# Adapter's up product on two row halves, biases by VectorE, inverse begun by pairs, one pool for the experts' tiles

## The chip, the cores and the metric

The kernel runs on one core of one Trainium2 chip. The time is device microseconds for one execution of the whole program; the median of several executions is compared. All data are fp32. The engines are named as in the profile: PE (TensorE, matmuls; PEld are its weight loads), DVE (VectorE), ACT (ScalarE), POOL (GpSimd) and SP, which here only issues DMAs.

## The reference, cut to what matters

There are 16 batches of 1024 tokens with 256 features. A block of Nystrom attention is followed by a feed-forward with one expert per batch; each is added to the input after a layer norm.

```python
x = x + LN(attn(LN(x)))
x = x + LN(ffn(LN(x)))

# attn: 16 heads of 16 features, 64 landmarks per head
Q_l, K_l = landmark means of Q, K
kernel1, kernel2, kernel3 = softmax(Q K_l^T), softmax(Q_l K_l^T), softmax(Q_l K^T)
SV = (kernel1 @ iterative_inv(kernel2)) @ (kernel3 @ V);  out = SV @ w_proj

def iterative_inv(K):                       # K: 64x64 per head
    V = K^T / max over columns of sum over rows of K
    for _ in range(6):
        KV = K @ V
        V = 0.25 * V @ (13 I - KV @ (15 I - KV @ (7 I - KV)))
    return V

# ffn on x: 8 experts, hidden 64
base = x @ W_base + b_base      # sum over d of x[t, d] W_base[d, o]
losses = mean((relu(x Wd1[e] + bd1[e]) Wd2[e] + bd2[e] - x)^2)   # per batch and expert
idx = argmin(losses)                                             # one expert per batch
a = relu(x Wa_down[idx] + ba_down[idx])                          # 64 wide
y = base + a Wa_up[idx] + ba_up[idx]
```

The kernel folds the layer norms' means into centred weights: rows of w_proj, W_base and the chosen expert's up weights and biases have their mean subtracted (`centre`), so that only the mean square of y is left to be found.

## The kernel before, in words

Each batch goes through stages: *a* (norm, transposes `pt_a`, Q and K `pq`, V `pv`, kernel3's maxima `psm`, weights `psc` and products `put`, ending in `u`), *p* (kernel2 and its inverse), *c* (kernel1, attention output, projection `po`, residual `x`), *d1* (norm, transposes `pt_d`, the losses of eight experts, choice and gathers), *d2* (the chosen adapter and the output). There are four streams, one for each of a, p, c and d1+d2, and each runs through the batches in order.

The order in which the streams' steps are issued is found while the program is built, by a planner (`Model`, `planned`, lines 1134 to 1264). Each step says before its code what it will take: `mm(us, mode, n)` a piece on PE with its tile shape (`full`, `r32`, `q64` and others) and its count of PE instructions, `ew(engine, us, behind, mark)` a piece on another engine. With these the planner tries orders ahead and keeps the one that loses PE the least. PE, ACT, DVE and POOL then run their instructions in the emitted order; an engine that waits holds all that is behind it. PSUM is used as four buffers of two banks (`ps2`); a step takes one for each product and a piece marked `free` gives it back.

*Stage p* (lines 540 to 737). 16 heads of 64x64 lie as 8 pairs over 128 rows. `kp` spreads the landmark means by pair with a mask (4 DVE multiplications, L596), so that `pk` (L600) is two full matmuls of 256 columns; DVE takes the maxima and subtracts (L608, L610), ACT takes the exponent, DVE normalizes (L614 to L617). `pkt` turns the matrices with 64-square matmuls against an identity. The starting scale comes from sums of columns (`cs`, L625), a PE transpose (`pcs`, L628), a maximum and its reciprocal on 8 rows (L630 to L634) and a transpose back (`prd`, L637); then `vi` is scaled (L641). In the first iteration `pkv` multiplies (L678) and also transposes `vi` by the identity to get `vt` (L680, L686). `across` (L658) copies the parts of a matrix that are needed on the other half of the rows into a second tile of the same size.

*Stage d1* (lines 932 to 1059). Per batch 16 tiles `df` of 128x1024: PE makes `pr`, DVE subtracts x (L995), ACT squares and sums twice (L998). `df` has a pool of three buffers; `xn_d` and the outputs `y_d` have a pool `yd` of two. After the choice POOL issues five gathers with the row numbers in `row` (L1040): two for `wdn`, one for `bdn`, and for `wup` 64 rows of up weights and two copies of the expert's bias row. SP loads b_base as a further row of `wup` (L1056). DVE centres the 67 rows (L1058).

*Stage d2* (lines 1061 to 1096). `pad` is the down product, with the two halves of the tokens on the two halves of PSUM's rows; ACT puts both through relu into rows 0 to 63 of `a_t` (L1078). POOL fills rows 64 to 66 of `a_t` with 0.5, 0.5 and 1.0 (L1065, L1066), so that the bias rows of `wup` are added by the same matmul. Then, twice per batch, for four chunks of 128 tokens:

```python
for k in range(NC):
    nc.tensor.matmul(po[:, j, :], lhsT=xt[:, k, cols], rhs=wbase_sb[:, k, :], start=(k == 0), stop=False)
nc.tensor.matmul(po[:, j, :], lhsT=a_t[:, cols], rhs=wup, start=False, stop=True)
```

`taken` (L299) copies the result to SBUF on ACT (L302) and sums its squares there (L306); POOL makes the reciprocal root (L260, L262), DVE scales and adds the residual (L295), SP stores.

Of the kernel before, what the change touches and what calls it, by code (L numbers as in the profile page):

```python
# [8 lines left out]
F32 = mybir.dt.float32  # L9
# [6 lines left out]
P = 128  # L16
# [29 lines left out]
def kernel(  # L46
# [89 lines left out]
    bd1_rows = work.tile([E // 2, P], F32, tag="df", name="bd1_rows", bufs=3)  # L136
    nc.scalar.dma_start(out=bd1_rows, in_=bd1.rearrange("(i r) h -> i (r h)", r=2))
    bd2_rows = work.tile([E * NC, P], F32, tag="df", name="bd2_rows", bufs=3)
# [19 lines left out]
    nc.gpsimd.memset(ones, 1.0)  # L158
    nhalf = const.tile([P, 4], F32, name="nhalf")
# [8 lines left out]
    pairmask = groups("pairmask", PC)  # L168
# [130 lines left out]
    def taken(b, at, h, po, tag):  # L299

        y = buf4k(tag, [P, 4, D], f"y_{at}{b}_{h}")
        nc.scalar.copy(y, po)  # L302
# [19 lines left out]
    def stage_a(b):  # L322
# [39 lines left out]
        for t0 in range(0, NT, 4):  # L362
# [20 lines left out]
            if t0 == 0:  # L383
                yield go(
                    ("a", b, "bd"),
                    [("a", b, "qk", i, c) for i in range(2) for c in range(NC)] + ([("p", b - 1, "kp")] if b >= 1 else []),
# [153 lines left out]
    def stage_p(b):  # L540
# [23 lines left out]
        def product(dst, a, c, to, rest):  # L564
# [4 lines left out]
            for g0 in range(2):  # L569
                for g1 in range(2):  # L570
                    four = [h for h in heads if h[rest[0]] == g0 and h[rest[1]] == g1]
                    for h in sorted(four, key=lambda h: (h[frm] ^ h[to], h[frm])):
# [3 lines left out]
                        yt = y[h[y_at[0]] ^ h[y[2]]] if isinstance(y, tuple) else y  # L576
# [14 lines left out]

        yield step("kp", ew("dve", 0.8, None))
        lm, bd = live[b].pop("lm"), live[b]["bd"]
        kp = inv.tile([P, NC, PC, M], F32, tag="yx", name=f"kp_{b}")
        for p in range(PC):
            nc.vector.tensor_scalar(kp[:, :, p, :], lm[:, 1], pairmask[:, p : p + 1], None, ALU.mult)  # L596
        yield step("k2", mm(1.3, "full", 8), ew("dve", 1.25, -1, "free"), ew("act", 0.5))
        pk = one_bank([P, NP, M], f"pk_{b}")
        for c in range(NC):
            nc.tensor.matmul(  # L600
                pk[:, c * PC : (c + 1) * PC, :].rearrange("x p l -> x (p l)"),
                lhsT=bd[:, c, :, :].rearrange("f r l -> f (r l)"),
                rhs=kp[:, c].rearrange("f p l -> f (p l)"),
                start=True,
                stop=True,
            )
        mx = small.tile([P, NP], F32, tag="mx2", name=f"mx2_{b}", bufs=1)
        nc.vector.tensor_reduce(mx, pk, X, ALU.max)  # L608
        k2 = mat("vt", "k2")
        nc.vector.tensor_tensor(k2, pk, last(mx, M), ALU.subtract)  # L610
# [7 lines left out]
        yield step("k2t", mm(Q, "q64", 64), ew("act", 0.5, -1, "free"), ew("dve", 0.6))  # L618
# [20 lines left out]
        nc.scalar.copy(rd, prd)  # L639
        vi = mat("vi")  # L640
        nc.vector.tensor_tensor(vi, k2t, last(rd, M), ALU.mult)  # L641
        v_at = kt_at

# [667 lines left out]
```

## Time and profile before

| | |
|---|---|
| median of 6 runs | 2366.25 us (2361.93 to 2375.11) |
| the profiled execution's time | 2361.97 us |
| its span, first to last instruction | 2360.2 us |
| PE, DVE, ACT, POOL busy | 2161.2, 1425.0, 1317.8, 271.9 us |
| mean granted clock of PE | 0.98 |
| base matmuls of d2 (L1088) / up matmuls (L1089), busy | 134.9 / 78.2 us |
| y_d copies by ACT (L302), 32 | 32.4 us |
| fills of a_t by POOL (L1065, L1066), 16 each | 17.5 and 15.4 us |

Busy time of PE is the union of its matmuls. These are pipelined, and what one costs is seen best from the distance between starts. Idle time of an engine is told with what ended it.

### The profile page before, as it was taken

The numbers are of one execution on the slowest core, as the hardware profiler recorded it, in microseconds if no ns is written. First come the engines' busy times: TensorE is split into PE (matmuls) and PEld (weight loads), VectorE is DVE, ScalarE is ACT, GpSimd is POOL, SyncE is SP. The second block draws the span as 40 slices with busy tenths as digits, with TensorE's granted clock in tenths as the row PEclk, the third lists the DMA queues.
The fourth block names the chain that finished last, engine by engine and source line by source line (L and its number), as shares of the span: only waits on it lengthen the run. The fifth ranks groups of instructions, "written<-read, shape, count | busy, mean of one in ns | idle before, by whom it ended". The sixth has DMA issues, their size and how long they took to land.

```text
span 2360.2 us, 85848 instructions
## 1 busy us (share of the span) xinstructions
PE 2161.2 (92%) x39346; PEld 1381.3 (59%) x39346; DVE 1425.0 (60%) x2715; ACT 1317.8 (56%) x2659; POOL 271.9 (12%) x387
## 2 busy tenths in 40 slices
PE   7999999999899999999999999999999999898965
PEld 4666565565655766556565656657556465665542
DVE  6556565756456666665666667575665656475633
ACT  2345655645655556464665656565464655666635
POOL 1001020110200202021020200202011020111021
PEclk9999999999999999999999999999999999999878
DMA  3000001010010100101010010101001010010000
GB/s 112 20 21 21 2 20 41 5 56 2 13 47 3 58 2 14 46 5 55 2 58 2 14 46 3 58 2 48 12 5 56 2 40 2 6 38 20 22 21 21
DMA packets 56626, 60.36 MB, mean 26 GB/s; under 512 B 4996, under 2 KB 55240, under 8 KB 56264
## 3 DMA queue, kind: packets, MB, share of 16 engines
q1 hardware_dynamic: 50240, 50.35, 6.8%
q8 instruction: 309, 5.06, 0.9%
q0 software_dynamic: 2560, 2.14, 0.4%
q10 hardware_dynamic: 3464, 2.37, 0.3%
q14 instruction: 53, 0.43, 0.1%
HBM read 38.08 MB, written 16.78 MB: 23 GB/s over the span
## 4 chain that ended last, share of the span: by engine, by line
PE 41%; DVE 9%; ACT 7%; issue 3%; POOL 2%; DMA 0%; POOLq 0%; DVEq 0%; ACTq 0%
PE ph L954 6%; PE pq L351 5%; PE pr L987 4%; PE pf L1088 3%; ACT df L998 3%; PE po L881 3%; DVE df L995 2%; PE pf L1089 2%; PE pv L372 2%; PE psv L833 2%; PE psct L804 2%; PE psct L812 1%; PE psm L420 1%; PE pb L577 1%; PE psc L766 1%
## 5 line engine op out<-in xcount | busy, mean ns | idle before, releaser
L998 ACT ACTIVATE df<-df,bd_sb 128x512 f32<-128x512 f32 x512 | 363.2, 710 | 128.1 <-DVE df L995 127.1
L995 DVE TENSOR_TENSOR df<-pr,xt_d 128x1024 f32<-128x1024 f32 x256 | 302.8, 1217 | 83.6 <-PE pr L987 48.6
L987 PE MATMUL pr<-ht,wd_sb 64*64 64x512 f32 x2048 | 252.2, 597 | 6.8 <-ACT e L822 2.5
L954 PE MATMUL ph<-xt_d,wd_sb 128*128 128x512 f32 x512 | 238.1, 608 | 1.0 <-ACT e L822 0.7
L351 PE MATMUL pq<-xt_a,wqkv_sb 128*128 128x512 f32 x512 | 229.9, 599 | 0.0
L429 DVE TENSOR_REDUCE mx<-psm 128x2 f32<-128x1024 f32 x128 | 149.9, 1216 | 46.4 <-PE psm L420 46.2
L774 DVE TENSOR_REDUCE maxima<-psc 128x16 f32<-128x1024 f32 x128 | 150.1, 1215 | 27.6 <-PE psc L766 27.4
L954 PEld LDWEIGHTS ph<-xt_d,wd_sb 128*128 128x128 f32 x512 | 93.7, 192 | 115.8 <-issue 97.7
L822 ACT ACTIVATE e<-psct 128x1024 f32<-128x1024 f32 x128 | 123.5, 1016 | 66.9 <-PE psct L812 65.0
L351 PEld LDWEIGHTS pq<-xt_a,wqkv_sb 128*128 128x128 f32 x512 | 94.2, 190 | 108.2 <-issue 102.4
L465 ACT ACTIVATE e<-psc 128x1024 f32<-128x1024 f32 x128 | 122.7, 1021 | 32.9 <-PE psc L455 32.6
L1088 PE MATMUL pf<-wbase_sb,xt_d 128*128 128x256 f32 x512 | 134.9, 386 | 1.3 <-ACT xx L683 1.3
L881 PE MATMUL po<-wproj_sb,svt 128*128 128x256 f32 x512 | 122.1, 393 | 6.3 <-ACT vt L707 3.0
L260 POOL TENSOR_SCALAR ve_c_y<-ss_c 128x4 f32<-128x4 f32 x32 | 6.2, 195 | 1026.2 <-ACT square_c L306 1026.0
L692 DVE TENSOR_TENSOR sq<-psq,eye 128x512 f32<-128x512 f32 x96 | 65.8, 686 | 93.4 <-PE psq L577 88.5
L698 DVE TENSOR_TENSOR t<-eye,pb 128x512 f32<-128x512 f32 x96 | 65.4, 681 | 91.7 <-PE pb L577 91.4
L295 DVE SCALAR_TENSOR_TENSOR y_d<-y_d,rstd_d_y,x 128x256 f32<-128x256 f32 x128 | 53.2, 479 | 107.0 <-POOL rstd_d_y L262 107.0
L987 PEld LDWEIGHTS pr<-ht,wd_sb 64*64 64x64 f32 x2048 | 64.5, 133 | 89.4 <-issue 47.0
L372 PE MATMUL pv<-wqkv_sb,xt_a 128*128 128x256 f32 x512 | 116.6, 382 | 0.2 <-ACT e L822 0.2
L962 ACT ACTIVATE ht<-ph,bd_sb 128x1024 f32<-128x1024 f32 x64 | 71.0, 1109 | 75.0 <-PE ph L954 74.6
L881 PEld LDWEIGHTS po<-wproj_sb,svt 128*128 128x128 f32 x512 | 97.5, 195 | 25.3 <-ACT svt L856 4.1
L372 PEld LDWEIGHTS pv<-wqkv_sb,xt_a 128*128 128x128 f32 x512 | 95.6, 190 | 19.2 <-issue 5.0
(183 smaller groups left out, 4115.9 us busy)
## 6 DMA issues: line engine op xcount, KB each, us to landing
out_dram<-y_d SPq DMA_DIRECT2D x32, 512.0 KB
x<-in_L_attn_x_dram SPq DMA_DIRECT2D x15, 1024.0 KB
xa<-in_L_attn_x_dram SPq DMA_DIRECT2D x15, 1024.0 KB
xa<-in_L_attn_x_dram SPq DMA_DIRECT2D x2, 512.0 KB
x<-in_L_attn_x_dram SPq DMA_DIRECT2D x2, 512.0 KB
wqkv_sb<-in_L_attn_w_qkv_dram ACTq DMA_DIRECT2D x1, 768.0 KB
wd_sb<-in_L_ffn_Wd_dram ACTq DMA_DIRECT2D x2, 256.0 KB
wd_sb<-in_L_ffn_Wd_dram ACTq DMA_DIRECT2D x1, 512.0 KB
```

The lines of the kernel that those rows point to most:

```text
L351: nc.tensor.matmul(pq[:, n, :], lhsT=wqkv_sb[:, k, f0 : f0 + P], rhs=xt[:, k, n * 512 : (n + 1) * 512], start=(k == 0), stop=(k == NC - 1),)
L372: nc.tensor.matmul(pv[:, j, :], lhsT=xt[:, k, (t0 + j) * P : (t0 + j + 1) * P], rhs=wqkv_sb[:, k, 2 * D : 3 * D], start=(k == 0), stop=(k ...
L429: nc.vector.tensor_reduce(mx3[:, n, q : q + 2], psc[g], X, ALU.max)
L465: nc.scalar.activation(e, psc[g], AF.Exp)
L774: nc.vector.tensor_reduce(mx[:, t0 : t0 + 2, 64 * g : 64 * g + 64].rearrange("x t (p j) -> x p t j", p=2)[:, :, :, 0 : 2 * NC], psc[g].rea ...
L822: nc.scalar.activation(e, psc[g], AF.Exp)
L881: nc.tensor.matmul(po[:, j, :], lhsT=svt[n][:, c, j * P : (j + 1) * P], rhs=wproj_sb[:, c, :], start=(c == 0), stop=(c == NC - 1),)
L954: nc.tensor.matmul(ph[:, n, :], lhsT=wd1_sb[:, k, 2 * i : 2 * i + 2, :].rearrange("p e h -> p (e h)"), rhs=xt[:, k, n * 512 : (n + 1) * 51 ...
L987: nc.tensor.matmul(pr[to, r, :], lhsT=wd2_sb[half, i, k * P + 64 * f : k * P + 64 * f + 64], rhs=ht[half, cols], start=True, stop=True,)
L995: nc.vector.tensor_tensor(df, pr, middle(xt[:, k, cols], 2), ALU.subtract)
L998: nc.scalar.activation(df[:, r, :], df[:, r, :], AF.Square, bias=bd2_sb[:, e, k : k + 1], accum_out=part[:, e, k * NW + n : k * NW + n + 1],)
L1088: nc.tensor.matmul(po[:, j, :], lhsT=xt[:, k, cols], rhs=wbase_sb[:, k, :], start=(k == 0), stop=False)
```

## The change

*Adapter.* `pad`'s moving operand now takes even chunks of 128 tokens (f = 0) into one half of the rows and odd chunks into the other, and ACT's relu writes them to the same two halves of `a_t`, which is [128, 512] and has no rows of ones. `wup` is [128, 2, 256]: part 0 has the up weights on both halves of the rows (a gather of 128 rows), part 1 the expert's bias on all 128 rows (a gather of 128 rows, all alike); DVE adds b_base, which is loaded once for all rows (`bbase_sb`), and centres both parts. The eight base matmuls of a half come first, then four up matmuls, each on 64 rows, even chunks into one bank and odd chunks into the other. `taken` no longer copies y_d with ACT: DVE adds the bias from `wup[:, 1]` on the way out of PSUM. The two fills by POOL and SP's load of b_base per batch are gone.

*Inverse.* `kp` is gone: `pk` is eight matmuls of 32 rows and 64 columns into two PSUM buffers, and maxima and subtraction come in two parts. One matmul with `in_half` (ones within each half of the rows) gives all sums of columns on all rows; a DVE maximum and a reciprocal give the scale `rd`. `vt` is k2 scaled in place; the first product is k2t by k2t, with the scale applied after it by DVE (`xh`), from which `y` is taken. The transposes and ACT copies for `rrow`, `rd`, `vi` and the first `vt` are gone. `across` makes a tile of half the size.

*Pools.* `df`, `xn_d` and `y_d` share one pool of four buffers (`yd`). The two small bias tables of the start lie in stage c's pool `e1`, and the first step of stage c follows the step that reads them. The steps' figures for the planner follow the new work, and a piece on PE can now be told to take no PSUM buffer.

```diff
@@ start
+    bbase_sb = const.tile([P, D], F32, name="bbase_sb")
+    nc.scalar.dma_start(out=bbase_sb, in_=b_base.unsqueeze(0).to_broadcast([P, D]))
-    bd1_rows = work.tile([E // 2, P], F32, tag="df", name="bd1_rows", bufs=3)
+    bd1_rows = work.tile([E // 2, P], F32, tag="e1", name="bd1_rows")
...
+    in_half = const.tile([P, P], F32, name="in_half")
+    nc.gpsimd.memset(in_half, 0.0)
+    for _, half in halves():
+        nc.gpsimd.memset(in_half[half, half], 1.0)
-    pairmask = groups("pairmask", PC)
@@ taken
-        y = buf4k(tag, [P, 4, D], f"y_{at}{b}_{h}")
-        nc.scalar.copy(y, po)
+        y = buf4k(tag, [P, 4, D], f"y_{at}{b}_{h}", 4 if tag == "yd" else 2)
+        if bias is None:
+            nc.scalar.copy(y, po)
+        else:
+            nc.vector.tensor_tensor(
+                y.rearrange("p (i f) d -> p f i d", f=2), po, bias.unsqueeze(1).unsqueeze(1).to_broadcast([P, 2, 2, D]), ALU.add
+            )
@@ stage_p
-        yield step("kp", ew("dve", 0.8, None))
-        for p in range(PC):
-            nc.vector.tensor_scalar(kp[:, :, p, :], lm[:, 1], pairmask[:, p : p + 1], None, ALU.mult)
-        pk = one_bank([P, NP, M], f"pk_{b}")
+        pk = [two_banks([P, 2, 512], f"pk_{b}_{g}") for g in range(PC // 2)]
         for c in range(NC):
+            for p in range(PC):
+                nc.tensor.matmul(
+                    pk[p // 2][:, p % 2, c * M : (c + 1) * M],
+                    lhsT=bd[rows32(p), c, :, :].rearrange("f r l -> f (r l)"),
+                    rhs=lm[rows32(p), 1, c, :],
...
+        pcs = one_bank([P, NP, M], f"pcs_{b}")
+        nc.tensor.matmul(
+            pcs.rearrange("x q m -> x (q m)"), lhsT=in_half, rhs=k2.rearrange("x q m -> x (q m)"), start=True, stop=True
+        )
         kt_at = product(pkt[0], (k2, NATURAL), (eye, None), "t", ("p2", "s"))
+        nc.vector.tensor_reduce(cs, pcs, X, ALU.max)
+        nc.vector.reciprocal(rd, cs)
         nc.scalar.copy(k2t, pkt[0])
-        nc.vector.tensor_reduce(cs, k2t, X, ALU.add)
-        nc.tensor.transpose(pcs.rearrange("q r m -> q (r m)"), cs, ident)
...
-        nc.tensor.transpose(prd, rrow.rearrange("q r m -> q (r m)"), ident[:NP, :NP])
-        nc.scalar.copy(rd, prd)
-        nc.vector.tensor_tensor(vi, k2t, last(rd, M), ALU.mult)
+        vt, vt_at = k2, NATURAL
+        nc.vector.tensor_tensor(vt, k2, last(rd, M), ALU.mult)
...
+                first = (k2t, kt_at) if i == 0 else (vi, v_at)
+                x_at = product(px, (k2t, kt_at), first, h, (g, "p2"))
                 if i == 0:
-                    vt_at = product(pvt, (vi, v_at), (eye, None), h, (g, "p2"))
...
+                    nc.vector.tensor_tensor(
+                        xh.rearrange("x (u p) m -> x u p m", p=2), by_pair, last(rd_by_pair, M), ALU.mult
+                    )
+                    nc.vector.tensor_tensor(y, xh, middle(eyes[0], NP), ALU.subtract)
@@ stage_d1
-                    df = buf4k("df", [P, 2, 512], f"df_{b}_{i}_{k}_{n}", 3)
+                    df = buf4k("yd", [P, 2, 512], f"df_{b}_{i}_{k}_{n}", 4)
...
+        wup = small.tile([P, 2, D], F32, tag="wup", name=f"wup_{b}", bufs=1)
+        gather(wup[:, 0, :], wa_up.rearrange("e r o -> (e r) o"), 4)
+        gather(wup[:, 1, :], ba_up, 3)
-        nc.sync.dma_start(out=wup[R + 2 : R + 3, :], in_=b_base.unsqueeze(0))
+        nc.vector.tensor_tensor(wup[:, 1, :], wup[:, 1, :], bbase_sb, ALU.add)
+        for i in range(2):
+            centre(wup[:, i, :])
@@ stage_d2
-        nc.gpsimd.memset(a_t[R : R + 3, :], 1.0)
-        nc.gpsimd.memset(a_t[R : R + 2, :], 0.5)
...
+                    rhs=xt[:, k, :].rearrange("p (i f t) -> p f i t", f=2, t=P)[:, f],
...
+        for f, half in halves():
+            nc.scalar.activation(a_t[half, :], pa[half, f, :], AF.Relu, bias=bdn[half])
...
-            yield go(("d", b, "po", n), [("d", b, "a")], mm(5.2, "full", 48), *NORMED)
+                mm(3.44, "full", 32),
+                mm(0.9, "r64", 16, None),
...
+            po = two_banks([P, 2, 2, D], f"pf_{b}_{n}")
+            for i in range(2):
+                for f in range(2):
+                    t = 4 * n + 2 * i + f
+                    for k in range(NC):
+                        nc.tensor.matmul(
+                            po[:, f, i, :],
+                            lhsT=xt[:, k, t * P : (t + 1) * P],
+                            rhs=wbase_sb[:, k, :],
...
+            for i in range(2):
+                for f, half in halves():
+                    cols = slice((2 * n + i) * P, (2 * n + i + 1) * P)
+                    nc.tensor.matmul(po[:, f, i, :], lhsT=a_t[half, cols], rhs=wup[half, 0, :], start=False, stop=(i == 1))
+            ys.append(taken(b, "d", n, po, "yd", wup[:, 1, :]))
```

## The prediction

> **What bounds the kernel now.** I read the page first: engine totals, then the slices.
>
> ```profile
> span 2360.2 us, 85848 instructions
> PE 2161.2 (92%) x39346; PEld 1381.3 (59%) x39346; DVE 1425.0 (60%) x2715; ACT 1317.8 (56%) x2659; POOL 271.9 (12%) x387
> PE   7999999999899999999999999999999999898965
> PEclk9999999999999999999999999999999999999878
> ```
>
> PE is busy nearly everywhere; only the first slice and the last five or so are thinner. The table by stretch of time sizes this (PE, PEld, DVE, ACT, POOL busy, granted clock, DMA):
>
> ```profile
> 0.00:118.00 118.00, 96.00 (x1260) 59.69 (x1264) 70.79 (x150) 36.52 (x48) 9.79 (x29) 1.00 0.22 66
> 118.00:2124.00 2006.00, 1887.48 (x35852) 1217.09 (x35848) 1245.60 (x2357) 1152.99 (x2309) 226.25 (x312) 0.99 0.08 24
> 2124.00:2242.00 118.00, 104.69 (x1806) 62.55 (x1801) 67.50 (x116) 75.58 (x175) 13.93 (x19) 0.93 0.07 21
> 2242.00:2360.00 118.00, 72.98 (x460) 41.96 (x452) 41.07 (x94) 52.67 (x130) 21.98 (x28) 0.82 0.06 21
> ```
>
> In the 2006 us of the middle PE is busy 94% (1887.5), DVE 62%, ACT 57%: there a microsecond off PE is worth most of a microsecond. The last 118 us have PE busy for 73, at 0.82 of the clock: that stretch is a chain from engine to engine. So I price middle and tail apart.
>
> PE's timeline, where the work to be changed stands beside work that already uses parts of the array (start, length, line, x records; a fp32 matmul leaves two records):
>
> ```profile
> 328.65 1.04 PE L812 MATMUL psct<-mt,minus_max 32*128 32x512 f32 x8
> 329.51 1.04 PE L444 MATMUL psc<-mrow,ones 32*128 32x512 f32 x8
> 330.37 1.07 PE L455 MATMUL psc<-bd,kt 32*128 32x128 f32 x32
> 331.37 0.69 PE L577 MATMUL psq<-yx 64*64 64x64 f32 x32
> ...
> 336.90 1.03 PE L1088 MATMUL pf<-wbase_sb,xt_d 128*128 128x256 f32 x4
> 337.76 0.60 PE L1089 MATMUL pf<-wup,a_t 67*128 67x256 f32 x2
> 338.20 1.03 PE L1088 MATMUL pf<-wbase_sb,xt_d 128*128 128x256 f32 x4
> ```
>
> Read starts, not lengths: lengths overlap. Two base matmuls take 0.86 us (336.90 to 337.76), one up matmul 0.44 though it fills 67 rows. Four 32-row matmuls of 512 columns take 0.86 together (328.65 to 329.51); sixteen of 128 columns take 1.00 (330.37 to 331.37), which is 4 x 0.215 and about 0.14 for the change to 64-square tiles.
>
> The tail, around the last but one batch's output product (DVE works in order):
>
> ```profile
> 2255.57 1.01 ACT L302 COPY y_c<-po 128x1024 f32<-128x1024 f32 x1 [3.81 <-PE po L881]
> 2260.20 1.67 DVE L295 SCALAR_TENSOR_TENSOR x<-y_c,rstd_c_y,x 128x256 f32<-128x256 f32 x4 [3.77 <-POOL rstd_c_y L262]
> 2262.22 1.22 PE L1089 MATMUL pf<-wup,a_t 67*128 67x256 f32 x2 [3.76 <-POOL a_t L1066]
> 2274.04 1.67 DVE L295 SCALAR_TENSOR_TENSOR y_d<-y_d,rstd_d_y,x 128x256 f32<-128x256 f32 x4 [12.16 <-POOL rstd_d_y L262]
> 2279.14 1.67 DVE L295 SCALAR_TENSOR_TENSOR y_d<-y_d,rstd_d_y,x 128x256 f32<-128x256 f32 x4 [3.44 <-POOL rstd_d_y L262]
> 2285.67 3.65 PE L288 MATMUL pt_d<-ident,xn_d 128*128 128x128 f32 x16 [11.20 <-DVE xn_d L232]
> ```
>
> The last batch's rows are ready at 2261.9, but its statistics stand on DVE behind both y_d, at 2280.7. Between them lies batch 14's product, which waited 3.76 us for POOL's fills of a_t.
>
> **The parts, on PE.**
>
> *Up product.* Now 128 matmuls of 0.435 us. After: eight per batch, as pairs on rows 0-63 and 64-127 into two banks. If a pair overlaps as the four 32-row tiles do, it takes the time of one: 64 x 0.435 = 27.8 us less. The ends are 0 (no overlap) and 27.8; the 64-square tiles of L987 (1024 matmuls of 512 columns in 252.2 us, 0.98 per four against 0.86 for one) are nearest, with two row halves into two banks, so I take 27.8 and keep the 0.1 per group for the switches. Of this 3.5 lies in the last two batches and is counted with the tail: 24.3 here.
>
> *Inverse, scores.* Two 256-column matmuls (0.86 us) become eight of 32 rows and 64 columns. By the 128-column row four take 0.215; at 64 columns between 0.11 and 0.215, so 0.22 to 0.43 for eight. Middle: 0.54 less, x16 = 8.6 (7 to 10).
>
> *Inverse, scale.* Two small transposes go (pcs 4.4 us busy, prd 3.3) and one 512-column full matmul comes, 0.86 x 16 = 13.8: 6.1 more.
>
> *First product.* The transposing matmuls of v0 go: 16 matmuls, 10.7 us busy at most, at the 64-square pace of four rounds of 0.107 us (half the 128-column row) 6.9. I take 6.9.
>
> *Fills of a_t.* POOL no longer writes the ones rows (two fills, 1.09 and 0.96 us a batch). PE waited 9.9 us for them in all, 4.6 of that in the middle: 4.6 less.
>
> *Changes of tile shape.* The planner's new order, counted by the shapes on PE, has 951 changes against 913. At 0.13 each (0.14 above; 2300.31 to 2300.43 later in the trace, the end of ph by its pace to pr's start): 38 x 0.13 = 5 more. Bounds 2 to 8.
>
> The Trainium skill speaks against this part: "TensorEngine Tiling (Array Packing)", Key Properties, says that a change of tiling mode drains the array. The page "TensorE: Matmul & The Clock Gate", Single matmul latency, gives an undrained stream N/2.4 ns and a lone matmul (398 + N)/2.4; an estimate from it is 166 ns per change, so 6.3 us in place of 5. Row and page disagree by 1.3 us only.
>
> Sum on PE in the middle: -24.3 - 8.6 + 6.1 - 6.9 - 4.6 + 5 = -33.3 us.
>
> **The parts beside PE.** DVE: 32 additions of the bias from PSUM replace ACT's copies; nearest is L995, also PSUM plus a repeated operand, at 1217 ns: 39 us more. wup: one addition (419 ns, as L493) and two centrings (0.41 + 0.15 + 0.35) in place of one, 2.2 us a batch for 1.1: 18 more. The inverse on DVE: kp 13.8, cs 10.9, cmx 4.4, rrow 3.4, rmx 2.4 go; the maximum from pcs 10.9, the scaled xh 11, split scores some 5, a reciprocal 3 come: 5 less. DVE goes to about 1477 us, 63%. ACT loses y_d's copies (32.4), vt's (9.5), one xx a batch (9.4), rd (2.6): 54 less. POOL loses 33 of fills; two gathers grow to 128 rows, priced by wdn's (1031 ns against 914 and 890): 4 more. Their landing, 2.4 us now, is at most wdn's 2.8 to 3.1, apart from 190 KB more bytes, 0.7 us at the 281 GB/s of the first 20 us; up stands behind eight base matmuls (3.4 us) instead of two, which covers that and the longer centring. In the sum these are nothing, because DVE and ACT have over a third of the middle idle; if that cover were gone, DVE's 52 us would be the price. SP loses 16 loads of 1 KB that held its queue 521 us behind gathers; the loads behind them made DVE wait only 7.6 us in all, mostly at the start: nothing. At the start: one more broadcast load of 128 KB (0.5 us at 281 GB/s, behind wbase) and three short fills (0.2 each by L158), off the first chain. The bias transposes already stood before stage c's first use; nothing. The shared pool: df has four buffers instead of three and shares them with xn_d and y_d. 36 allocations a batch divide by four, so a next batch's first two df wait for y_d's stores, where now xn_d does, which comes earlier; DVE shows no wait for these stores. DVE waited 13.0 us for ACT's df and 11.9 behind square_c, which a fourth buffer can ease: nothing to 5 less, taken as nothing.
>
> **What of it reaches the end.** The middle was 6% idle, partly because the inverse's short steps wait for DVE and ACT, whose work doesn't shrink in step. I let 0.8 of the 33.3 through: 27. Ends: a quarter (8), and all plus a little (37), since three steps of the inverse's serial chain (kp, rrow, v0) also go.
>
> *Tail.* DVE's order is unchanged in kind: x, both biases, both y_d, then the statistics. Batch 14: relu ends 2260.0; the first base half runs from 2257.4 to 2260.9 without the fill; up 1.0 to 2261.9; second half 3.5 and 1.0 to 2266.4; DVE 1.2 to 2267.7; squares 2.2 and POOL 1.3 to 2271.4; y_d 1.67 to 2273.1. That is 7.6 before 2280.7; 7 taken. Last batch: the same steps save about 3 of the 12 us of PE from 2335.8 to 2348.1. Tail -10 (-5 to -13).
>
> **Sum.** -27 - 10 = -37 against the profiled execution's 2361.97: 2325. That execution is 4.3 below the median of the six, 2366.25; the same step from the median gives 2329. Runs spread from 2361.9 to 2375.1, and 0.3% (7 us) is what can be told from no change.
>
> **Rivals.**
> 1. *PE's time comes off and turns into waits.* For: in the middle the inverse waits in turn for DVE, and DVE takes on 52 us. Against: DVE 62%, ACT 57%. Then a quarter of 33 and 5 to 10 of tail: 2348 to 2356, or no change in the worst.
> 2. *Slower: the bias addition blocks DVE.* ACT today waits 114.8 us, 32 times, for pf. This wait moves to DVE, where the reductions that free PSUM are queued behind it; PE then stands for banks. It decides where over 37 of the 115 us reach PE; with half, +57 - 37: 2386. Against: DVE already waits 91 us for pb and 89 for psq in order, and PE still ran at 94%.
> 3. *The pairs don't overlap.* The 27.8 are gone, in the tail 2 of 10: 2361.97 - 7 - 8 + 4.3, about 2351. L804, L812 and L987 speak against it.
> 4. *More than the sum.* The shorter chain lets a third of the middle's 118 idle us go: 2290.
>
> **How the numbers follow.** Forecast 0.68 (own range 2312 to 2345), rival 1 0.14, rival 2 0.08, rival 3 0.04, rival 4 0.06. Likeliest 2329. From 2300 to 2357 all but rival 2, most of 4 and the worst of 1 are held. Faster by over 0.3%: 0.68 + 0.04 + 0.06 + 0.08 of rival 1 = 0.86; the other 0.06 of rival 1 is within; slower 0.08.
>
> **What would show it.** Right: the up matmuls at about 0.9 to 1.0 us per four, no wait for a_t's fills, PE busy near 2125, DVE 1470 to 1480, statistics of the last batch starting some 7 us after y_d's sooner, PE still over 92% in the middle. Wrong: up matmuls at 1.7 per four (rival 3); long DVE waits on pf with PE idle on banks after them (rival 2); PE's share falling to 92% with DVE's waits grown (rival 1). I'd be wrong most easily in the order: the planner lays all streams anew, and a few gaps over a microsecond more or less in each batch are as large as my sum.

## The result, and the profile after

The changed kernel takes 2357.35 us (median of 20 runs, 2350.08 to 2363.04), the kernel before 2366.81 us in the runs made beside it: a ratio of 0.9961, with a 95% interval of 0.9951 to 0.9970. That is 9 us or 0.4% faster. The forecast was 2329 us. The sign was right and three quarters of the gain did not come.

The page of the changed kernel: span, busy time of each engine, and PE with its granted clock in 40 slices.

```profile
span 2351.4 us, 84954 instructions
...
PE 2143.6 (91%) x39026; PEld 1359.3 (58%) x39026; DVE 1469.2 (62%) x2762; ACT 1268.4 (54%) x2579; POOL 240.8 (10%) x358
...
PE   6988989999899999899999899999989999888975
...
PEclk9999999999999999999999999999999999989988
```

PE's busy time fell by only 17.6 us (2161.2 to 2143.6), DVE's rose by 44 and ACT's fell by 49 (forecast: 52 and 54). PE's row shows an 8 in slices 3, 4, 6, 11, 17, 23 and 30, where before all of these but slice 11 were 9. The same four stretches as in the prediction, now of the changed kernel:

```profile
0.00:118.00 118.00, 94.60 (x1263) 61.42 (x1263) 68.82 (x138) 34.14 (x44) 9.80 (x30) 0.96 0.22 67
118.00:2124.00 2006.00, 1875.02 (x35349) 1195.35 (x35353) 1281.38 (x2395) 1113.17 (x2244) 199.14 (x285) 0.98 0.08 25
2124.00:2242.00 118.00, 104.68 (x1978) 64.57 (x1972) 70.68 (x124) 72.61 (x168) 13.53 (x19) 0.94 0.08 23
2242.00:2351.00 109.00, 69.32 (x460) 37.92 (x459) 48.31 (x106) 48.53 (x126) 18.31 (x24) 0.83 0.08 26
```

In the same 2006 us of the middle PE has fewer matmuls (35349 records against 35852) and is busy for 1875.0 us instead of 1887.5; its granted clock is 0.98 instead of 0.99. It did not run ahead: the time went into idle and into half clock.

The groups of the changed work, with line, shape and count, then busy time and mean ns, then the idle time just before:

```profile
L1114 PE MATMUL pf<-wbase_sb,xt_d 128*128 128x256 f32 x512 | 120.1, 388 | 0.0
L310 DVE TENSOR_TENSOR y_d<-pf,wup 128x1024 f32<-128x1024 f32 x32 | 39.0, 1223 | 87.0 <-PE pf L1124 87.0
L1124 PE MATMUL pf<-wup,a_t 64*128 64x256 f32 x256 | 36.3, 402 | 0.0
L645 PE MATMUL pcs<-k,in_half 128*128 128x512 f32 x32 | 17.1, 617 | 2.7 <-DVE k L639 2.0 <-DVE maxima L792 0.8
L617 PE MATMUL pk<-lm,bd 32*128 32x64 f32 x256 | 11.4, 288 | 0.7 <-DVE mx L439 0.7
```

The up product (L1124) is busy for 36.3 us where it was 78.2, and PE no longer waits ahead of it (11.3 us before, 9.9 of them for POOL's fills of a_t). Measured from start to start and without the idle time behind them, the up matmuls took 58.4 us before and take 34.0 now; four of them, 1.74 us before at 0.435 each, now take 1.06.

The tail. The timeline of the changed kernel, last batch's projection first, then batch 14's adapter (start, length, instruction, idle time before it):

```profile
2251.45 5.59 PE L899 MATMUL po<-wproj_sb,svt 128*128 128x256 f32 x16 [1.10 <-ACT svt L874]
2258.84 3.72 PE L1114 MATMUL pf<-wbase_sb,xt_d 128*128 128x256 f32 x16
2262.49 1.14 PE L1124 MATMUL pf<-wup,a_t 64*128 64x256 f32 x8
2263.56 3.72 PE L1114 MATMUL pf<-wbase_sb,xt_d 128*128 128x256 f32 x16
...
2268.39 1.22 DVE L310 TENSOR_TENSOR y_d<-pf,wup 128x1024 f32<-128x1024 f32 x1 [3.49 <-PE pf L1124]
...
2273.24 1.67 DVE L300 SCALAR_TENSOR_TENSOR y_d<-y_d,rstd_d_y,x 128x256 f32<-128x256 f32 x4 [2.05 <-POOL rstd_d_y L267]
...
2279.75 1.51 PE L293 MATMUL pt_d<-ident,xn_d 128*128 128x128 f32 x6 [11.41 <-DVE xn_d L237]
```

The first four up matmuls take 1.07 us (2262.49 to 2263.56), and PE does not wait ahead of them. The last y_d of batch 14 starts at 2273.24 (2279.14 before), and `pt_d` of the last batch at 2279.75 (2285.67 before). But the last batch's projection started at 2251.45, and before it was 2251.82: with nearly all of the middle done, the changed kernel was ahead by only 0.4 us.

So I split each trace at the start of the last of the projection's matmuls, and the time up to there into three: PE idle (no matmul running), the loss by half clock (half of PE's busy time in stretches where the granted clock was half), and the rest, which is PE's work as it would be at full clock.

| us | up to there | PE idle | lost by half clock | rest | from there to the end |
|---|---|---|---|---|---|
| before | 2255.2 | 158.0 | 26.0 | 2071.1 | 105.0 |
| after | 2256.7 | 171.4 | 39.5 | 2045.7 | 94.8 |

In this order PE's work is down by 25.4 us and the tail by 10.2 (8.4 if the tail is counted from the projection's first matmul). Idle (+13.4) and half clock (+13.5) gave the 25.4 back. The split is not exact. Two kernels below with the same PE instructions in the same order differ by 5.8 us in the rest, and the changed kernel's own instructions in the old order (x1) have 2059.1 there, 13.4 more: only 12.0 of the 25.4 are seen in both orders.

### The profile page after: what moved, and what is told of

It reads as the page before. It is cut to its first block, busy times and chain, and to the rows that moved or that the text cites. A ratio compares the mean times of both kernels' runs of the same rounds, so it can differ in the third digit from the quotient of the medians.

```text
span 2351.4 us, 84954 instructions
## 1 busy us (share of the span) xinstructions
PE 2143.6 (91%) x39026; PEld 1359.3 (58%) x39026; DVE 1469.2 (62%) x2762; ACT 1268.4 (54%) x2579; POOL 240.8 (10%) x358
## 5 line engine op out<-in xcount | busy, mean ns | idle before, releaser
L1114 PE MATMUL pf<-wbase_sb,xt_d 128*128 128x256 f32 x512 | 120.1, 388 | 0.0
L851 PE MATMUL psv<-w_bd,e 128*32 128x34 f32 x8192 | 91.1, 199 | 30.1 <-issue 23.6
L851 PEld LDWEIGHTS psv<-w_bd,e 128*32 128x32 f32 x8192 | 80.7, 110 | 56.5 <-issue 35.6
L316 ACT ACTIVATE square_d<-y_d 128x256 f32<-128x256 f32 x128 | 53.3, 417 | 108.8 <-DVE y_d L310 100.8
L1114 PEld LDWEIGHTS pf<-wbase_sb,xt_d 128*128 128x128 f32 x512 | 95.9, 192 | 18.4 <-issue 4.4
```

Of the source, the lines that this page charges most:

```text
L851: nc.tensor.matmul(psv[rows32(g), j // 2, col : col + 2 * (HD + 1)], lhsT=es[p // 2][:, p % 2, j * P + 32 * g : j * P + 32 * g + 32], rhs= ...
L1114: nc.tensor.matmul(po[:, f, i, :], lhsT=xt[:, k, t * P : (t + 1) * P], rhs=wbase_sb[:, k, :], start=(k == 0 and i == 0), stop=False,)
```

## The experiments

Two explanations stood at first. Either the work of the changed steps cannot come off the end, because something else takes its place (the chain through DVE, the bias addition), or it can, and the newly planned order of all steps lost it. Experiments x1 to x12 ran on three chips on which the kernel before took 2361.7 to 2363.5 us. x13 to x18 fell on two chips where the kernel before itself took 2430.9 and 2436.2 us, so from those only ratios to the kernel before on the same chip are compared.

### The new work in the old order (x1)

The changed kernel with the planner replaced by the list of steps that the kernel before was given; the steps `kp`, `rrow` and `v0`, which no longer exist, are left out of the list.

```diff
-    order, emitted = planned(), streams()
+    order = [int(c) for c in (
+        "0000000000300200120200102221000000000101000100010000000100010011010001001000101010101001010010101012"
...
+    )]
+    emitted = streams()
```

> The changed kernel's instructions, issued in the order that the planner found for the kernel before: steps kp, rrow and v0 are dropped from that list, and in batches 2, 4, 5 and 9 the step k2 stands where kp stood; nothing else of the work differs from the changed kernel. In the changed kernel the stretch to the last projection of the last batch took as long as before (2251.4 against 2251.8 us from the start), so the middle gave nothing. Theory O (the new order fits worse and ate the middle's 27 us): in the old order the work comes off, 2325 to 2340 us. Theory W (the new work itself brings waits, DVE above all, in any order): 2350 to 2365, no better than the changed kernel.

2347.18 us, ratio 0.9935 [0.9918, 0.9951]: 16 us faster than before. The tail is the same 94.8 us; up to the last projection it is 2248.2 us, with idle of 159.5 and 29.5 lost by half clock, close to the kernel before (158.0 and 26.0). So the new planned order costs about 6 us (by the ratios, whose intervals touch at 0.9951) to 10 us (by the medians) against the old one for the same instructions. But 16 is not 37: the order is one part only. In the old order too, just 7.0 us came off up to the last projection.

### The up product left out (x2)

```diff
-                    nc.tensor.matmul(po[:, j, :], lhsT=xt[:, k, cols], rhs=wbase_sb[:, k, :], start=(k == 0), stop=False)
-                nc.tensor.matmul(po[:, j, :], lhsT=a_t[:, cols], rhs=wup, start=False, stop=True)
+                    nc.tensor.matmul(po[:, j, :], lhsT=xt[:, k, cols], rhs=wbase_sb[:, k, :], start=(k == 0), stop=(k == NC - 1))
```

> The kernel before, same order, with the up matmuls (L1089) left out, so the adapter's up product and its biases are missing from the output; gathers, fills and all else stay. It measures what PE time taken off the middle is worth. Up matmuls and the wait before them were 69 us of PE's time between starts, 61 of it in the first fourteen batches. If the conversion of 0.8 that I assumed holds: 2366 - 0.8 x 61 - about 12 in the tail, some 2305. If freed PE time mostly turns into waits (rival 1): 2340 to 2352.

2292.45 us, 0.9699 [0.9680, 0.9718]: 71 us less. From start to start the output product (base and up) took 196.1 us of PE before and takes 124.9 here, 71 less: 58 of up matmuls and 11 of waits ahead of them, most for POOL's fills. The page of this kernel:

```profile
span 2290.6 us, 85284 instructions
...
PE 2102.2 (92%) x39090; PEld 1333.4 (58%) x39090; DVE 1423.6 (62%) x2715; ACT 1317.5 (58%) x2659; POOL 271.8 (12%) x387
```

PE stays at 92% and DVE at 62%. With the order kept and nothing added elsewhere, a microsecond off PE in this place is a microsecond off the end. Rival 1 as a law of the kernel falls, and my factor of 0.8 was too low for it. The run adds no work to DVE, so what DVE's new work costs is left to x3 and x12.

### The bias addition left out (x3)

The changed kernel in its own order; ACT copies y_d from PSUM as before.

```diff
-            ys.append(taken(b, "d", n, po, "yd", wup[:, 1, :]))
+            ys.append(taken(b, "d", n, po, "yd"))
```

> The changed kernel in its own order, but y_d is copied out of PSUM by ACT as before and the adapter's and base's biases are left out of the output; DVE loses 32 additions (about 39 us), ACT gains 32 us. If DVE's added load and its waits for pf (87 us, 26 times) cost the middle, it becomes 10 to 25 us faster than the changed kernel: 2332 to 2347. If DVE's load is off the path: within 5 us of 2357.

2348.94 us, 0.9945 [0.9926, 0.9965]. Against the changed kernel's 0.9961 [0.9951, 0.9970] the intervals overlap; by the ratios 4 us are the addition's, and by the ends of the intervals no more than 10. In the groups above DVE's addition follows 87.0 us of waiting for `pf`; that wait did move from ACT (114.8 us before) to DVE, and it costs little. Rival 2 falls.

### Each part alone in the old order (x5, x6, x9, x10, x11)

All have the list of x1, or the list of the kernel before where no step was dropped. x5 has the adapter's edits of the diff alone, x11 the same and the shared pool; x6 has the inverse's edits alone; x9 of these only the scores by pairs (the edits from `k2` to the subtraction), x10 only the scale and the first product (the edits from `pcs` on). The cores of x9 and x10:

```diff
-        kp = inv.tile([P, NC, PC, M], F32, tag="yx", name=f"kp_{b}")
...
+        pk = [two_banks([P, 2, 512], f"pk_{b}_{g}") for g in range(PC // 2)]
         for c in range(NC):
+            for p in range(PC):
+                nc.tensor.matmul(
+                    pk[p // 2][:, p % 2, c * M : (c + 1) * M],
```

```diff
+        nc.tensor.matmul(
+            pcs.rearrange("x q m -> x (q m)"), lhsT=in_half, rhs=k2.rearrange("x q m -> x (q m)"), start=True, stop=True
+        )
...
-        nc.tensor.transpose(prd, rrow.rearrange("q r m -> q (r m)"), ident[:NP, :NP])
```

> The adapter's part alone (pairs of up matmuls, bias by DVE, no fills, no load of b_base), inverse and pools as before, every step in the order found for the kernel before. Without the up matmuls that order gave 71 us for 69 us of PE's time. The new work in the old order has 44.5 us between starts for the up matmuls where there were 69.4, and 7 us less for the base matmuls among them: if the adapter's part carries the whole gain at that rate, 32 us less than before, some 2331 to 2335. If its DVE additions bring waits in this order, or the inverse's part is what gave the 16 us of that run: 2345 or more.

> The inverse's part alone, adapter and pools as before, in the old order with kp, rrow and v0 dropped (and k2 in kp's place in batches 2, 4, 5 and 9). My forecast had it at 9 us less on PE plus a shorter chain: 2352 to 2360. If it takes back what the adapter gives in the old order (32 less 16): 2370 to 2382.

> Of the inverse's part only the scores by pairs (pk as eight 32-row matmuls into two PSUM buffers, maxima and subtraction in two parts, no kp), all else as before, old order without kp. The whole inverse's part cost 19 us in the old order. Its pk took 18.4 us of PE between starts there against 15.6 before, where I had forecast 8.6 less. If the scores carry the cost: 2372 or more. If the scale and first product carry it: 2358 to 2366.

> The rest of the inverse's part alone: sums by the in_half matmul, vt scaled in place, first product of k2t with itself and the scale after it, half-size across tile; pk and kp as before; old order without rrow and v0. By PE's time between starts pcs and prd give 5.6 more and pkv 5.4 less. If the scale carries the 19 us (y of the first iteration comes one DVE pass later, 0.69 us, and the 0.86 us matmul stands in front of pkt): 2372 or more; if not: 2358 to 2366.

> The adapter's part with the one pool of four buffers (df, xn_d, y_d), bias tables in e1, inverse as before, old order. Against the adapter alone (2340): if the shared pool is free, within 4 us of it; if the fourth df buffer eases DVE, up to 5 us faster; if df waits for the stores of y_d, slower, 2346 or more.

| kernel | median us | ratio to before, 95% | up to last projection | PE idle | half clock | rest | after it |
|---|---|---|---|---|---|---|---|
| x5 adapter | 2339.86 | 0.9902 [0.9884, 0.9919] | 2249.1 | 155.7 | 42.2 | 2051.2 | 94.9 |
| x11 adapter, pool | 2340.64 | 0.9892 [0.9874, 0.9911] | 2244.6 | 155.8 | 31.8 | 2057.0 | 94.7 |
| x6 inverse | 2380.52 | 1.0086 [1.0062, 1.0111] | 2272.4 | 165.1 | 34.6 | 2072.7 | 105.3 |
| x9 scores | 2377.99 | 1.0059 [1.0036, 1.0081] | 2261.8 | 168.2 | 23.4 | 2070.2 | 105.4 |
| x10 scale, first product | 2364.09 | 1.0006 [0.9989, 1.0024] | 2258.7 | 154.5 | 26.7 | 2077.5 | 104.6 |

The columns from the fourth on are of one profiled execution each, which need not be a middling one: x5's took 2345.93 us, 6 above its median, and x9's 2369.01, 9 below.

Three readings. The adapter's part is worth some 22 to 25 us, and the whole gain of the tail is in it (94.9 against 105.0). The shared pool makes no difference that can be told. The inverse's part makes the kernel slower by 19 us in the old order, and the scores by pairs carry most of it: 14 us, against a forecast gain of 8.6. Beside the adapter the inverse costs less: from x5 (0.9902) to x1 (0.9935) it is 8 us.

Do the weight loads explain why the scores do not gain? The tile `pk` in the kernel before, and then in x9 (duration of one record as least, median and most, in ns):

```profile
L600 PEld LDWEIGHTS pk<-kp,bd x64: 186/190/190, 40.2 to 2085.3; 128*128 128x128 f32 x64
```

```profile
L603 PEld LDWEIGHTS pk<-lm,bd x256: 181/185/187, 39.8 to 2088.0; 32*128 32x128 f32 x128
```

A load of 32 rows lasts as long as one of 128 rows, and there are four times as many. The Trainium skill, "TensorE: Matmul & The Clock Gate", LDWEIGHTS (loading the stationary operand), says that a load's time is set by its columns and not by its rows, which is what 185 beside 190 ns shows. It says P / 1.2 ns, 107 ns for 128 columns, where these records show 181 to 190; records of 32 and 64 columns (`psv`, `pr`) last 109 and 133 ns at the median. From 64 to 128 columns these are 54 ns more, which is the page's rate, with some 80 ns on top at every width.

But the loads do not stand one behind the other. In the traces of x9 and of the changed kernel, loads on the four groups of 32 rows mostly start 5 to 8 ns apart, the next four about 0.09 us later, and so do their matmuls. Where nothing comes between, a batch's `pk` takes 0.60 us or less from its first start to the next instruction's: in seven of x9's sixteen batches and in twelve of the changed kernel's, against 0.86 to 1.06 before. That is a gain, though not the forecast one.

What takes it back is waiting. From start to start the `pk` matmuls took 15.6 us before, 18.8 in x9 and 12.9 in the changed kernel's own order; the forecast had 5.2 (13.8 less 8.6). Without the idle time behind them it is 15.6, 12.6 and 11.0. In two batches of x9 PE stands for about 2 us behind `pk`, for an exponent of ACT or for DVE's maxima, of another stage.

In x9's trace, whose execution is 7 us longer than the kernel before's, PE's idle time up to the last projection is up by 10.2 us on 158.0; the rest is not higher than before. That the old order, fitted to one `pk` product in one PSUM buffer, suits two products in two buffers badly would be a reason; it is argued, not shown.

### The planner's horizon (x4, x7, x8, x12 to x15)

The planner looks ahead by `AHEAD` us. Changing this figure changes no instruction, only the order. x4 and x14 are the changed kernel with 55 and 85, x8 and x13 the kernel before, x15 and x12 the adapter's part alone; x7 is the adapter's part alone at 70.

```diff
-AHEAD, LAST, GAP = 70.0, 250.0, 1.0
+AHEAD, LAST, GAP = 85.0, 250.0, 1.0
```

> The changed kernel, its planner looking 55 instead of 70 us ahead: the same instructions in another order. Theory O says that orders of this planner scatter by 10 us or more, so it may land anywhere from 2335 to 2375. Theory W says that the order matters little: 2350 to 2362.

> The adapter's part alone, with the order that the planner finds for it with the changed figures. Theory O: the work of the old-order run, but an order drawn anew; anywhere from 2325 to 2375. Against theory O: within 5 us of the old-order run.

> The kernel before with its planner looking 55 instead of 70 us ahead: the same instructions in another order. The changed kernel moved by 39 us under this edit, with PE at half clock for 193 us instead of 123. Theory O: the kernel before moves as well, by 10 us or more, likely slower since 70 was there first. If only the new work is sensitive to its order: within 8 us of 2363.

> The adapter's part alone with its own order, the planner looking 85 us ahead. The same work gave 2340 in the old order and 2356 in its own at 70. Theory O: another draw, anywhere from 2325 to 2385; a value below 2335 would be the better version. If 70 is merely a good setting: above 2356.

> The kernel before, planner looking 85 us ahead. If 85 finds better orders for any work: 2335 to 2350, and the adapter's 2324 is 85's merit in part. If orders scatter without regard to the setting: anywhere from 2350 to 2390.

> The changed kernel, planner looking 85 us ahead. By the old order's prices (adapter 22 less, scores and scale 14 to 19 more) it should lie 14 to 19 above the adapter alone in orders of equal merit: 2338 to 2345 if 85 is a better setting; 2350 to 2395 if orders scatter.

> The adapter's part alone, planner looking 55 us ahead. Before and after were 25 and 39 us slower at 55 than at 70. If 55 is a worse setting for any work: 2375 to 2395. If orders scatter: anywhere from 2325 to 2390.

Ratios to the kernel before on the same chip; those marked * are from the chip where it took 2430.9 us:

| work | old order | horizon 55 | 70 | 85 |
|---|---|---|---|---|
| before | 1 | 1.0123 [1.0098, 1.0147] | 1 | 1.0049* [1.0029, 1.0068] |
| adapter alone | 0.9902 | 0.9920* [0.9890, 0.9950] | 0.9978 [0.9961, 0.9995] | 0.9837 [0.9815, 0.9858] |
| after | 0.9935 | 1.0133 [1.0109, 1.0157] | 0.9961 | 0.9910* [0.9877, 0.9944] |

On the three faster chips alone, the order moves the same work by 1.2% (before), 1.4% (adapter) and 2.0% (after): 29 to 47 us, where the whole change was to bring 37. No horizon is best for all three. The kernel before has its best order of the three at 70, the one it was given. Each edit of the steps draws another, and at 70 both the adapter alone (0.9978) and the changed kernel (0.9961) drew a worse one than the old list (0.9902 and 0.9935). Set against the kernel before at the same horizon, the change is 0.1% slower at 55 (1.0133 by 1.0123), 0.4% faster at 70 and 1.4% faster at 85 (0.9910 by 1.0049, on one chip). Which of these a run of the planner meets is luck.

In the extreme of x4 the clock shows what a bad order does:

```profile
span 2396.4 us, 84953 instructions
...
PEclk9999999998989999899899999999999999989988
```

Its work is that of the changed kernel, but slices in the middle fall to 8. From the trace, 180.1 us up to the last projection are idle and 68.7 are lost by half clock, where the changed kernel has 171.4 and 39.5: 8.7 us more of idle time go with 29.2 us more lost through the clock.

x12, the adapter's part alone at 85, takes 2324.4 us, 39 us less than before: it beats both kernels. Its page:

```profile
span 2320.8 us, 85736 instructions
...
PE 2143.3 (92%) x39346; PEld 1364.7 (59%) x39346; DVE 1473.3 (63%) x2811; ACT 1285.1 (55%) x2627; POOL 241.3 (10%) x355
...
PEclk9999999999999999999999999999999999999888
```

DVE has its 1473 us here too. Up to the last projection PE is idle for 141.3 us, 30 less than in the changed kernel, and loses 24.9 by half clock.

### The wait for wup's gathers (x16, x17, x18)

What in the new order loses the time? One candidate was in the waits of the changed kernel (total, times, longest):

```profile
DVE wup L1075 <- DMA wup<-in_L_ffn_ba_up_dram,row: 52.9, 12, 9.6
...
PE psv L851 <- issue: 23.6, 16, 4.5
```

Before, the wait for `wup` was 27 us in two rows:

```profile
DVE mean L153 <- DMA wup<-in_L_ffn_ba_up_dram,row: 21.1, 9, 8.1
...
DVE mean L153 <- DMA wup<-in_L_ffn_Wa_up_dram,row: 5.8, 1, 5.8
```

The timeline around 1757 us shows it harming PE:

```profile
1752.90 0.68 DVE L710 TENSOR_TENSOR sq<-psq,eye 128x512 f32<-128x512 f32 x1
...
1757.67 0.95 POOL L1058 DMA_INDIRECT wup<-in_L_ffn_ba_up_dram,row  x1 [0.30 <-issue]
...
1761.26 0.42 DVE L1075 TENSOR_TENSOR wup<-wup,bbase_sb 128x256 f32<-128x256 f32 x1 [7.68 <-DMA wup<-in_L_ffn_ba_up_dram,row]
...
1763.41 0.42 DVE L503 TENSOR_TENSOR ut<-put,ut 128x256 f32<-128x256 f32 x1
...
1763.88 0.43 PE L493 MATMUL put<-e,v_ones 128*32 128x64 f32 x6 [4.31 <-DVE ut L503]
```

DVE stands 7.68 us for the gather that POOL issued last; the centring of the two parts follows; `ut` stands behind it, and PE waits 4.31 us for `ut`. PE's idle time from the start of such a wait to 3 us after it, summed over the waits before 2150 us, is 14.8 us in the changed kernel and 16.5 in x7, against 6.0 in x1 and 4.4 in x5, the same work in the old order; 3.0 in x12, and 0.8 in the kernel before. Only x4, with 2.7, does not fit. So the seven instructions were moved behind the relu, with all other engines' instructions left in place.

```diff
         yield go(("d", b, "wup"), [("d", b, "gather")], ew("dve", 1.3, None))
-        nc.vector.tensor_tensor(wup[:, 1, :], wup[:, 1, :], bbase_sb, ALU.add)
-        for i in range(2):
-            centre(wup[:, i, :])
...
             nc.scalar.activation(a_t[half, :], pa[half, f, :], AF.Relu, bias=bdn[half])
+        nc.vector.tensor_tensor(wup[:, 1, :], wup[:, 1, :], bbase_sb, ALU.add)
+        for i in range(2):
+            centre(wup[:, i, :])
```

> The changed kernel in its own order on PE, ACT, POOL and SP; alone the seven VectorE instructions per batch that add b_base to wup and centre its two parts are issued later, with the adapter's relu instead of ahead of the down product. In the changed kernel VectorE stands 52.7 us in 11 waits for wup's gathers with other work queued behind it, and PE is idle for 14.8 us from the start of such a wait to 3 us after it, in the nine that lie before 2150 us (0.8 in the kernel before). Theory W: this wait is a good part of what the new order gave back; then 5 to 14 us come off the changed kernel's time, ratio to the kernel before 0.990 to 0.994. Theory P: PE's idle time there has other reasons and the order's loss lies elsewhere; then the ratio stays that of the changed kernel, 0.995 to 0.997.

> The same move in the adapter's part alone with the order that the planner makes for it at the horizon of 70. There one wait for wup of 9.47 us has PE idle for 8.9, and all such waits before 2200 us have 16.5 us of it. Theory W: 8 to 15 us come off, ratio 0.991 to 0.9945 where it was 0.9978. Theory P: 0.997 to 0.999.

> The same move in the adapter's part alone with the horizon of 85, where the waits for wup have PE idle for only 3.0 us. Theory W: 0 to 3 us, ratio 0.982 to 0.984. Theory P: 0.984. If the later centring makes the up product wait, 0.984 to 0.987.

x16: 1.0007 [0.9992, 1.0022]; x17: 0.9939 [0.9919, 0.9958]; x18: 0.9896 [0.9872, 0.9921]. All three ran on the chip where the kernel before took 2436.2 us, and the kernels that they are to be compared with did not run there, so the ratios decide little: x17 is lower than x7's 0.9978, and x16 and x18 are higher than 0.9961 and 0.9837. The traces say more. The wait is gone; one row of it is left in x16, that of the last batch:

```profile
DVE wup L1094 <- DMA wup<-in_L_ffn_ba_up_dram,row: 9.6, 1, 9.6
```

But PE's idle time behind DVE, over the whole span, is 107.1 us in x16 and 106.3 in the changed kernel, 94.8 in x17 and 88.8 in x7, 98.3 in x18 and 87.5 in x12. Taking the wait away did not lessen it: PE stood elsewhere instead. In x17 the gap of 9.45 us that ended at 784 us is gone, and one of 4.72 us ends at 486. The move also has a price of its own: in the tail the up product of batch 14 now waits 2.3 us for the later centring, and the time behind the last projection is 98.8 to 100.1 us in x16 to x18, where it is 94.7 to 95.4 in the same work without the move. So the three runs do not test the wait alone. My theory that it was a good part of the loss is not borne out.

The traces of x1 and of the changed kernel, the same instructions in two orders, point elsewhere. Up to the last projection PE's idle time behind DVE is 87.5 us in x1 and 88.9 in the changed kernel, hardly different. What differs is `issue`, time in which PE waited for nothing that the profile shows: 22.9 and 41.5 us (41.8 in x3, which has the changed kernel's order). Its largest row is that of `psv`, 23.6 us above; in x1 it is:

```profile
PE psv L851 <- issue: 6.2, 5, 1.9
```

Within a microsecond of the end of the three longest such waits of the changed kernel (4.54, 2.66 and 2.31 us, ending at 644.8, 1343.5 and 2023.0 us) a stretch of half clock begins as well. No run took these waits away, so they are a lead and not a cause, and against the kernel before, with 36.2 us of `issue`, they explain little. What grew against the kernel before is the idle time behind DVE, 66.9 us there: by some 21 us with the new work in both orders, and also without the bias addition (88.0 in x3). In the old order less `issue` and no wait for the fills made up for it. Which feature of the order loses the time stays open.

## Why the prediction was right and wrong

- **The up product** ("-24.3 here", and 0.9 to 1.0 us per four matmuls): right in kind, a little small. The pairs overlap, and rival 3 falls; four matmuls take 1.06 us. Up to the last two batches, where the 24.3 were to come, 48.7 us (112 matmuls at 0.435) became 29.7 (28 groups at 1.06), 19.0 less. The difference is near the 5 us that the prediction added for changes of shape.
- **The tail** ("-10"): right, 105.0 us became 94.8, and x5 shows that it is the adapter's. The last batch's `pt_d` came 5.9 us sooner, for a forecast of some 7.
- **Fills of a_t** ("4.6 less"): right; POOL does not appear as a releaser of PE in the changed kernel.
- **The scale** ("6.1 more"): right, 10.4 us became 16.0 from start to start, +5.6, and with the first product it is free (x10). **The first product** ("-6.9"): right in sign, 45.7 became 35.0, -10.7. These distances hold PE's waits as well, 4.2 of the 10.4 and 7.7 of the 45.7.
- **The scores** ("8.6"): wrong. In the planned order they gained 2.7, and in the old order they lost 3 on PE and 14 in the time. The step that failed is "By the 128-column row four take 0.215; at 64 columns between 0.11 and 0.215": I scaled from a stream in steady state to 0.22 to 0.43 for eight, and an undisturbed batch takes 0.60 to the next instruction's start. And no wait was priced: two products in two buffers leave 6.2 us of idle time behind them in x9, where one product left none.
- **Changes of shape** ("951 changes against 913"): the traces have 953 against 924, 29 more where 38 were forecast. Of the figures that the prediction takes from the Trainium skill, "TensorE: Matmul & The Clock Gate", N/2.4 for a stream stands in the section "Back-to-back issue gap", with 2.5 ns on top, which changes its estimate by 0.1 us.
- **DVE, ACT, POOL**: right. DVE 1469.2 us for a forecast of 1470 to 1480; the addition took 1223 ns for a forecast of 1217. PE's busy time was to be near 2125 and is 2143.6, of which 13.5 are the half clock's.
- **The gathers' landing** ("at most wdn's 2.8 to 3.1, apart from 190 KB more bytes, 0.7 us"): too low. The trace gives the landing of two gathers of each kind: the bias rows took 3.6 us both times (2.1 and 2.3 before), the up weights 2.7 and 6.0 (2.4 and 2.6). DVE's wait for them doubled, though x16 shows no gain from taking it away.
- **What reaches the end** ("I let 0.8 of the 33.3 through: 27"): this is the step that failed by the most. Up to the last projection nothing came through: it began at 2251.45 us where it had begun at 2251.82. Of the 33.3, 4.6 were a wait and 28.7 PE's work. The work did fall by 25.4 in this order, and idle gave back 13.4 and half clock 13.5. Yet the factor is not a law of the chain, which I had taken it for: with the order kept, leaving 71 us out of PE gave 71 (x2). What failed is the assumption that work and order can be priced apart by one factor: each change of the steps is also a new order, and the order moves the same work by 1.2 to 2.0%. In the prediction this stood only as its last sentence; it should have been the range, and a case of its own. Rival 1 named the outcome that came closest (2348 to 2356). As a law x2 and x12 speak against it, but the waits for DVE that it named did grow, by some 21 us.

Step by step the runs have it so: the adapter in the old order takes off some 23 us (x5, 0.9902); the inverse and the pool beside it add 8 (x1, 0.9935), where the forecast had the inverse's parts on PE at 9.4 less; and the new order adds 6 (0.9961); by the intervals each of these differences has some 5 us of doubt. So the order is not the whole of the shortfall: the inverse's part has as large a share, and alone it cost 19 us in the old order. Why it costs so much is open: the scores are 14 of the 19, and of these PE's own time for `pk` shows 3. x6 and x9 also judge the inverse in an order that was fitted to its old chain. That the sum still came out below zero was in part luck, as the same change at a horizon of 55 shows.

## What to carry to other kernels

Where a planner lays the order, split every change into work and order by running the new work in the old order, and before that run the old work with a planner's figure changed: that spread (here 29 to 47 us) belongs in the range, and a forecast below it says little. Take the share of an engine's time that reaches the end from a run that leaves work out, not from the share of idle time. And do not price small matmuls by a stream in steady state alone: here the idle time behind the small product took back in the old order what its smaller matmuls gave.

## What the runs showed of the hardware

- The same program differed by 2.9 to 3.2% between chips: the kernel before took 2361.7 to 2363.5 us on three chips and 2430.9 and 2436.2 on two. On the latter two, PE's idle time put down to `issue` was 50.8 to 76.4 us in x13 to x18, against 22.9 to 48.1 us on the others, and the loss by half clock up to the last projection 63 to 71 us, against 23 to 44 (and 68.7 in x4). The kernel before was not traced on those two, so this compares different kernels.
- Stretches of half clock come in multiples of 3.4 us, but for the last, which the end cuts off. In the changed kernel's trace 7 of 17 are one such window; the longest, at 2067.5 us, lasted 20.5 us, six windows, while PE was busy for 16.0 of it. The Trainium skill, "TensorE: Matmul & The Clock Gate", Part 1, has full clock return after one busy window of about 3.4 us. This stretch agrees: PE was busy for 54 to 83% of each of the first five windows and for the whole of the sixth, and then full clock came back.
- Weight loads and matmuls on the four groups of 32 rows mostly start 5 to 8 ns apart (`pk` in x9 and in the changed kernel): four loads of 185 ns each do not take four times as long as one.
- A single wait of PE for nothing that the profile shows (`issue`) reached 4.54 us (`psv` at 644.8 us of the changed kernel's trace); before, the longest ahead of `psv` was 2.0 us.
